# A graph-attention layer on one core: pair sums by single-input reduces, two buffers for near logits, and sums turned a batch later

## The chip, the core and the metric

The kernel runs on one core of a Trainium2 chip. The metric is the device time of one execution in microseconds (us), given as the median of several runs; it is to be as low as possible. The engines of the core work side by side, each in the order of its own instruction queue, and meet at semaphores: PE (matrix multiply), DVE (vector), ACT (scalar, and activations such as exp), POOL (general purpose; here it issues the gathers), and SP (here it issues loads). ACT also issues some DMAs.

## The reference, cut to what matters

A graph of N = 12500 nodes with 128 features and E = 412500 edges, sorted by their destination `tgt`. Every edge has 64 features. Attention has H = 4 heads of HD = 32.

```python
h = relu(layernorm(x))                                    # 12500 x 128
hn = (h @ W_node.T).reshape(N, H, HD)
e  = (edge_attr_64 @ W_edge.T).reshape(E, H, HD)
att = sum(concat([hn[src], hn[tgt], e], -1) * a, -1)      # E x H
att = where(att > 0, att, 0.2 * att)
m = maximum(segment_max(att, tgt), 0)
ex = exp(att - m[tgt])
denom = segment_sum(ex, tgt) + (E - deg)[:, None] * exp(-m)
out = x + segment_sum((ex / denom[tgt])[..., None] * hn[src], tgt)
```

So a logit is the sum of three parts: one of the source node, one of the destination node (below: the near logit, since destinations of neighbouring edges lie near each other) and one of the edge (below: z).

## The kernel before

**Tiling.** The edges are cut into 461 chunks of 896 (T = 7 tiles of 128), and 7 chunks make a batch: 66 batches. A table row in HBM holds 4 heads x 36 floats for each node: the 32 features of a head, a one, space, and the node's own logit. The loop of the program (L1121) runs over batches 0 to 64; the last batch, 65, is done in two parts behind it.

**One batch on the engines.** The queues' order is the order in which the functions are called in the loop, since each engine works its instructions in program order.

- *POOL* gathers the table rows of the batch's edges into one of RING = 4 buffers `hs` (L659): 49 indirect DMAs of 128 rows. Before each batch stands a memset of a tile called gate (L655), which waits until PE has finished the scatter of the batch that used the buffer last. In iteration b the gather of batch b+1 is issued, behind the scatter of batch b-3.
- *SP* loads, in iteration b, the near logits of batch b+1 (`load_near`, L605, 7 DMAs, each of which spreads one window of 32 nodes to all partitions), the node penalties of batch b+1 (L685; they mark where a node's edges begin) and the edge features of batch b+2 (`load`, L597).
- *PE* makes z of batch b+2 from the edge features at the end of iteration b (`begin`, L704 and L707, 14 matmuls).
- *ACT and DVE* pick each edge's near logit out of its window. ACT spreads the lower half of the window over all edges (`spread`, L618, tile `pick`); DVE halves it five times by predicated copies, by the bits of the edge's place (`choose`, L622 to L634). This is done in iteration b for batch b+1.
- *DVE and ACT* make the weights. `add_ends` adds the own logit and the near one (L758) and transposes (L760), so that a chunk and head lie on a partition; ACT copies the result to edge order (L763, four copies, one for each quadrant of 32 partitions). `highest_of` adds z (L771), applies the leak (L772, L773), finds the maximum of each node by two scans (L774, L776), subtracts it (L777) and forms a masked maximum (L778); four ACT copies (L780) take both results to `both`. `turn_weights` transposes back (L785), ACT takes exp (L790), and DVE writes the maxima into the rows (L791). `mark` (L716 to L722) writes the one-hot matrices of the scatter.
- *DVE and PE* scatter. DVE multiplies the rows by their weights (L859, three instructions) and adds tiles in pairs (L865, three adds), PE multiplies these sums by the one-hot matrices (L878, 10 products of 504 columns, each of which the trace shows as two matmuls). Where the two edges of a pair have different destinations, the second rows, masked by `split` (L868), are added up in two more adds (L870) and go through a correction matrix. PE accumulates all of it in `wide_ps`.
- *ACT* copies the accumulated sums of batch b-1 to `stage` (L886), writes them to HBM (`pass_on`, L887) and reads them back transposed (`turn_sums`, L900, 8 DMAs). `collect` (L915) waits for these and copies them into the input of the merge. Every two batches a merge on DVE (L946 to L988, called by `close`) joins neighbouring chunks' sums and adds them into the accumulators.

**Special places.** After batch COUNTED = 24 a count on DVE (L1006 to L1025) moves the accumulators' windows. From batch 62 on (`soon`) pass_on, turn_sums, collect and close are done for batch b itself in iteration b. Batch 65 takes `first_part` and `second_part`, which do not use `scatter` but multiply and add up chunk by chunk (L840, L847).

**Synchronization.** DMAs whose completion is counted by a semaphore of the kernel's own (near, pen, rows, wide, turned) are waited for by `landed`; all else is ordered by the framework, which makes a writer of a tile wait for its earlier readers, across engines by a semaphore.

Of the kernel before, what the change touches and what calls it, by code (L numbers as in the profile page):

```python
# [18 lines left out]
P = 128  # L19
# [50 lines left out]
PAIRS = ((0, 2), (2, 4), (4, T))  # L70
# [58 lines left out]
def kernel(  # L129
# [23 lines left out]
    wide = dram.tile([SB * BLOCK], F32, name="wide")  # L153
# [59 lines left out]
    lw = const.tile([P, CB, W * H], F32, name="lw")  # L213
# [14 lines left out]
    wide_sems, wide_done = [tc.alloc_semaphore("wide")], [0]  # L228
# [370 lines left out]
    def load_near(s):  # L599

        _, at = nc.values_load_multi_w_load_instructions(
            least_b[0:1, s.b, :s.chunks], engines=[ENG.SP], min_val=0, max_val=(NB * P - W) * NODE,
            skip_runtime_bounds_check_because="a dst is at most N, and N + W at most NB * P")
        for i, v in enumerate(at):
            by_itself(nc.sync.dma_start(  # L605
                lw[:, i, :].bitcast(U8),
                near_b[ds(v, W * NODE)].rearrange("(o c) -> o c", o=1).to_broadcast([P, W * NODE])),
                f"near{s.b}", near_sems, near_done, s.b % 2)

    def spread(s):  # L610

        landed(nc.scalar, f"near{s.b}", near_sems, near_done, s.b % 2, lw[:, :, :])
# [5 lines left out]
        nc.scalar.copy(s.pick[:, :, :s.chunks, :], lw[:, None, :s.chunks, :n].to_broadcast([P, T, s.chunks, n]))  # L618

    def choose(s):  # L620

        nc.vector.tensor_tensor(  # L622
# [51 lines left out]
    def landed(engine, group, sems, done, k, *what):  # L674

        wait = engine.wait_ge(sems[k], done[k], synchronizes=[engine.lower_ap(w) for w in what])
        if what:
            tc.declare_no_dep(wait.ins, group=group, reason="the semaphore counts these loads")
        tc.declare_fence(wait.ins, group=group)
# [67 lines left out]
    def grouped(s, what, g, t0, t1):  # L747

        order = "r w (t g i) -> r w g t i" if s.b == NBT - 1 else "r w (g i t) -> r w g t i"
        return what.rearrange(order, g=NQT, i=R)[:, :, g, t0:t1, :]  # L750
# [5 lines left out]
    def add_ends(s, t0, t1):  # L756

        nc.vector.tensor_tensor(logits[:, t0:t1, :s.chunks * H].rearrange("p t (q h) -> p t q h", h=H),  # L758
                                own_of(s, t0, t1), s.pick[:, t0:t1, :s.chunks, :H], op=OP.add)
        nc.vector.transpose(s.zst[:, t0:t1, :].rearrange("p t i -> p (t i)"),  # L760
                            logits[:, t0:t1, :].rearrange("p t i -> p (t i)"))
        for g in range(NQT):
            nc.scalar.copy(grouped(s, s.pair[:, 0:1, :], g, t0, t1)[:, 0], s.zst[g * R:(g + 1) * R, t0:t1, :])  # L763

    def highest_of(s, t0, t1):
# [5 lines left out]
        on_half(s, nc.vector.tensor_tensor(up[:, e0:e1], z, att[:, e0:e1], op=OP.add))  # L771
# [6 lines left out]
        nc.vector.scalar_tensor_tensor(mp, s.pen[:, e0 + 1:e1 + 1], -1.0 / BIG, up[:, e0:e1], op0=OP.mult, op1=OP.mult)  # L778
        for g in range(NQT):
            nc.scalar.copy(both[g * R:(g + 1) * R, :, t0:t1, :], grouped(s, s.pair, g, t0, t1))  # L780

    def turn_weights(s, t0, t1):
# [7 lines left out]
        nc.scalar.activation(ex_ps[:, t0:t1, :], ex_ps[:, t0:t1, :], AF.Exp)  # L790
# [35 lines left out]
    def second_part(s):  # L826
# [4 lines left out]
        r = work.tile([P, AW * (MC + 1)], F32, name="r")  # L831
        r = r[:, :AW * (len(spans) * s.chunks + 1)].rearrange("p (d c) -> p d c", d=AW)
        nc.scalar.copy(r[:, :, 1::len(spans)], s.first)
        nc.scalar.copy(r[:, :, 2::len(spans)], sum_part(s, *spans[1]))
        return r, s.breaks
# [16 lines left out]
    def scatter(s):  # L852
# [4 lines left out]
        for t0, t1 in PAIRS:  # L857
# [7 lines left out]
            nc.vector.tensor_tensor(tiles[:, t0, :], tiles[:, t0, :], tiles[:, t0 + 1, :], op=OP.add)  # L865
        add_to(s, t0, ROUNDS - 3)
        odd = s.hs.rearrange("p (t q) c -> p t q c", t=T)[:, 1::2, :, :]
        nc.vector.tensor_tensor(odd, odd, split_ps[:, :, :, None].to_broadcast([P, T // 2, CB, ROW]), op=OP.mult)  # L868
        for k in range(1, T // 2):
            nc.vector.tensor_tensor(tiles[:, 1, :], tiles[:, 1, :], tiles[:, 2 * k + 1, :], op=OP.add)  # L870
# [12 lines left out]
    def pass_on(s):  # L883
# [3 lines left out]
        by_itself(nc.scalar.dma_start(wide[:P * 2 * SPAN].rearrange("(p k) -> p k", p=P),  # L887
                                      s.stage.rearrange("p g c -> p (g c)")), f"wide{s.b}", wide_sems, wide_done, 0)

    def turn_sums(s):  # L890

        landed(nc.scalar, f"wide{s.b}", wide_sems, wide_done, 0)
# [12 lines left out]

    def collect(s):

        first, last = merge_of(s.b)
        if s.b == first:
            n = chunks_of(first, last)  # L910
            r = work.tile([P, AW * (MC + 1)], F32, name="r")
            merged[first] = r[:, :AW * (n + 1)].rearrange("p (d c) -> p d c", d=AW),
# [24 lines left out]
    def merge(b0, c0, count, r, breaks=None):  # L937

        n = count if breaks is None else 2 * count
# [7 lines left out]
        m = r[:, AW - 1, 1:n + 1]  # L947
        val = work.tile([P, CE], F32, name="up")[:, :AW * (n + 1)].rearrange("p (d c) -> p d c", d=AW)
# [6 lines left out]
        if not ended:  # L955
# [9 lines left out]
        nc.vector.tensor_copy(r[:, :AW - 1, 0], carry)  # L965
# [6 lines left out]
        part = r[:, :HD + 1, 1:n + 1]  # L972
        nc.vector.tensor_tensor(part, part, scale[:, None, :n].to_broadcast([P, HD + 1, n]), op=OP.mult)
        nc.vector.tensor_tensor_scan(val[:, :AW - 1, :].rearrange("p d c -> p (d c)"), f.rearrange("p d c -> p (d c)"),
                                     r[:, :AW - 1, :].rearrange("p d c -> p (d c)"), 0.0,
# [129 lines left out]
    with tc.manual_schedule():  # L1105
# [7 lines left out]
        load_near(batch(0))  # L1113
        load_pen(batch(0))
# [6 lines left out]
        for b in range(NBT - 1):  # L1121
# [5 lines left out]
            load_near(batch(b + 1))  # L1127
# [10 lines left out]
            if b + 2 < NBT:  # L1138
                open_rows(batch(b + 2))
            if b == NBT - 2:  # L1140
# [5 lines left out]
            if b < NBT - 2:  # L1146
                spread(batch(b + 1))
                mark(s)
# [32 lines left out]
            if soon:  # L1181
# [3 lines left out]
                collect(s)  # L1185
# [300 lines left out]
```

## Time and profile before

| | |
|---|---|
| median of 3 runs | 4788.1 us (4781.82 to 4800.94) |
| the profiled execution's own time | 4789.11 us |
| its span, from the first to the last instruction | 4787.3 us |
| busy: DVE | 3041.7 us (64%), 3240 instructions |
| busy: POOL | 3227.6 us (67%), 3394 instructions |
| busy: PE | 1287.3 us (27%), 2855 matmuls |
| busy: ACT | 801.2 us (17%), 988 instructions |
| mean granted clock of PE | 0.627 |
| gathers | 3223 indirect DMAs, 237.83 MB, 19.1% of the time of 16 DMA engines |

The profile shows one execution, instruction by instruction. A group is all instructions of one line of the code, engine and shape: its busy time, the mean duration of one in ns, the time the engine was idle just before them, and what ended most of that idle time ("<-DMA", another engine's instruction, "remote" for a semaphore whose sender the profile could not name, or "issue" where the engine waited for nothing that is shown). The timeline gives single instructions: start and duration in us, engine, line, and in brackets the idle time before and its releaser. Durations of PE are modelled at their ends. An engine with the suffix q is its instruction queue, here where it issues DMAs.

### The profile page before, as it was taken

Reading aid. Unit: us, or ns where it says so; the run is one execution under the profiler, and the core shown is the slowest. Engines: PE = TensorE matmul, PEld = TensorE weight load, DVE = VectorE, ACT = ScalarE, POOL = GpSimd, SP = SyncE. Lnnn points to the kernel's source line nnn. Section 1 sums busy time; section 2 is a strip of 40 time slices with the busy share of each in tenths; the row PEclk is TensorE's granted clock in tenths of the full one; section 3 lists DMA queues with packets and bytes.
Section 4 is the critical chain, followed back from the end, with each engine's and each line's share of the span. In section 5 each row is a group of like instructions: output and inputs, shape, how many; then the busy total and the mean of one; then the engine's idle time right before and its main releaser. Section 6 shows DMA issues by size and latency. Waiting matters only on the chain. (4 is left out here: it accounts for less than half of the span.)

```text
span 4787.3 us, 17028 instructions
## 1 busy us (share of the span) xinstructions
PE 1287.3 (27%) x2855; PEld 455.8 (10%) x2855; DVE 3041.7 (64%) x3240; ACT 801.2 (17%) x988; POOL 3227.6 (67%) x3394
## 2 busy tenths in 40 slices
PE   4312232222322314033321322322312313222221
PEld 3000010000100101011100100100100101010010
DVE  7644385586665767098945755846855748485576
ACT  3111021021111112022211211211211212121011
POOL 5777667667676767747776775775776767767630
PEclk7656566566656656566665666655656656566566
DMA  6433333343333424324342433333424323333330
GB/s 169 113 79 85 88 107 81 94 106 101 101 92 95 107 73 111 95 77 121 91 103 70 113 100 92 99 98 96 108 79 116 90 79 108 102 104 83 93 89 13
DMA packets 417217, 457.02 MB, mean 95 GB/s; under 512 B 240582, under 2 KB 324762, under 8 KB 417100
## 3 DMA queue, kind: packets, MB, share of 16 engines
q0 software_dynamic: 103136, 237.83, 19.1%
q1 hardware_dynamic: 199216, 165.73, 12.9%
q10 hardware_dynamic: 114748, 52.30, 4.1%
q14 instruction: 93, 0.76, 0.1%
q8 instruction: 24, 0.39, 0.0%
HBM read 406.51 MB, written 49.05 MB: 95 GB/s over the span
## 5 line engine op out<-in xcount | busy, mean ns | idle before, releaser
L659 POOL DMA_INDIRECT hs<-table,ends x3223 | 3193.1, 991 | 1009.9 <-issue 1002.7
L878 PE MATMUL pa<-hs,hot 128*128 128x504 f32 x1300 | 771.6, 753 | 2407.8 <-issue 791.8
L878 PEld LDWEIGHTS pa<-hs,hot 128*128 128x128 f32 x1300 | 301.3, 242 | 2841.3 <-issue 1877.1
L707 PE MATMUL z<-eft,wa 128*32 128x512 f32 (+1 forms) x792 | 377.6, 627 | 598.5 <-issue 389.6
L634 DVE COPY_PREDICATED pick<-more,lw 128x3136 f32<-128x3136 int32 x65 | 240.1, 3694 | 428.3 <-issue 324.1
L771 DVE TENSOR_TENSOR up<-z,a 32x896 f32<-32x896 f32 (+1 forms) x67 | 72.2, 1078 | 664.9 <-remote 512.8
L859 DVE TENSOR_TENSOR hs<-hs,exr 128x1848 f32<-128x1848 f32 (+1 forms) x195 | 466.5, 2392 | 0.0
L618 ACT COPY pick<-lw 128x3136 f32<-128x3136 f32 x65 | 182.3, 2805 | 1179.2 <-DMA lw<-near 948.5
L780 ACT COPY both<-a 32x448 f32<-32x448 f32 (+2 forms) x268 | 263.0, 982 | 247.8 <-DVE a L778 154.9
L634 DVE COPY_PREDICATED pick<-more,pick 128x1568 f32<-128x1568 int32 (+3 forms) x260 | 250.9, 965 | 8.9
L763 ACT COPY a<-zst 32x224 f32<-32x224 f32 (+2 forms) x268 | 155.6, 581 | 577.4 <-DVE logits L758 216.0
L865 DVE TENSOR_TENSOR hs<-hs 128x1008 f32<-128x1008 f32 x195 | 235.8, 1209 | 8.5 <-DVE hs L859 1.0
L655 POOL MEMSET gate<- 128x1 f32 x62 | 7.5, 121 | 339.8 <-remote 297.6
L868 DVE TENSOR_TENSOR hs<-hs,more 128x3024 f32<-128x3024 f32 x65 | 214.7, 3303 | 2.3
L704 PE MATMUL z<-eft,wa 128*64 128x512 f32 (+1 forms) x132 | 84.2, 727 | 375.8 <-issue 252.6
L707 PEld LDWEIGHTS z<-eft,wa 128*32 128x32 f32 x792 | 89.1, 123 | 920.8 <-issue 701.8
L886 ACT COPY stage<-pa 128x1008 f32<-128x1008 f32 x65 | 64.9, 998 | 609.0 <-remote 550.9
L870 DVE TENSOR_TENSOR hs<-hs 128x1008 f32<-128x1008 f32 x130 | 157.0, 1208 | 4.5
L986 DVE TENSOR_REDUCE up<-a 128x280 f32<-128x1960 f32 x66 | 145.1, 2198 | 4.2 <-DVE a L984 2.0
L984 DVE TENSOR_TENSOR a<-up,more 128x1960 f32<-128x1960 f32 x66 | 144.2, 2185 | 0.0
L774 DVE TENSOR_TENSOR_SCAN up<-pen_sb,z 32x896 f32<-32x896 f32 (+1 forms) x67 | 133.6, 1994 | 5.7 <-DVE z L773 2.6
L776 DVE TENSOR_TENSOR_SCAN a<-pen_sb,up 32x896 f32<-32x896 f32 (+1 forms) x67 | 132.6, 1979 | 2.3
(191 smaller groups left out, 1251.8 us busy)
## 6 DMA issues: line engine op xcount, KB each, us to landing
eft<-in_ef SPq DMA_DIRECT2D x33, 1792.0 KB
hs<-table,ends POOLq DMA_INDIRECT x3223
eft<-in_ef SPq DMA_DIRECT2D x33, 1344.0 KB
wide<-stage ACTq DMA_DIRECT2D x65, 504.0 KB
lw<-near SPq DMA_DIRECT2D x461, 64.0 KB
pen_sb<-pens SPq DMA_DIRECT2D x66, 98.1 KB
table<-rows ACTq DMA_DIRECT2D x9, 648.0 KB
xg<-in_x SPq DMA_DIRECT2D x52, 112.0 KB
```

What stands on the lines that cost most here:

```text
L618: nc.scalar.copy(s.pick[:, :, :s.chunks, :], lw[:, None, :s.chunks, :n].to_broadcast([P, T, s.chunks, n]))
L634: nc.vector.copy_predicated(s.pick[:, :, :s.chunks, :n], bit[:, :, :, None].to_broadcast([P, T, s.chunks, n]), more)
L659: load = nc.gpsimd.indirect_dma_start(out=s.hs[:, t * CB + q, :], out_offset=None, in_=table[:, :], in_offset=bass.IndirectOffsetOnAxis(ap ...
L707: s.made = own_half(s, nc.tensor.matmul(s.z[:, part], wa3[:, j + s.b % 2 * (SB + 1), :], s.eft[:, j, part], start=False, stop=(j == NEXT - ...
L763: nc.scalar.copy(grouped(s, s.pair[:, 0:1, :], g, t0, t1)[:, 0], s.zst[g * R:(g + 1) * R, t0:t1, :])
L780: nc.scalar.copy(both[g * R:(g + 1) * R, :, t0:t1, :], grouped(s, s.pair, g, t0, t1))
L859: nc.vector.tensor_tensor(rows, rows, ex_ps[:, t0:t1, :CB * H, None].to_broadcast([P, t1 - t0, CB * H, HB]), op=OP.mult)
L865: nc.vector.tensor_tensor(tiles[:, t0, :], tiles[:, t0, :], tiles[:, t0 + 1, :], op=OP.add)
L868: nc.vector.tensor_tensor(odd, odd, split_ps[:, :, :, None].to_broadcast([P, T // 2, CB, ROW]), op=OP.mult)
L870: nc.vector.tensor_tensor(tiles[:, 1, :], tiles[:, 1, :], tiles[:, 2 * k + 1, :], op=OP.add)
L878: scattered[s.b] = nc.tensor.matmul(wide_ps[:, g, :], s.hot[:, k, g * NEXT:g * NEXT + SB, :].rearrange("p q r -> p (q r)"), flat[:, at:at ...
L986: nc.vector.tensor_reduce(put, spread_out, AX.X, OP.add)
```

## The change

Four things are changed, all in the loop over batches.

1. *Sums in pairs.* `scatter` multiplies the odd seventh tile first and then the six others in one instruction. The three pair sums are made by one `tensor_reduce` over a view in which the two tiles of a pair are the innermost axis (4032 bytes apart), into `two`, which is the memory of `pick`; PE reads the pairs there. The rows that `split` has masked are summed by a second `tensor_reduce` (three tiles, 8064 bytes apart) into tile 0.
2. *No ACT copies around the weights.* z and the transposed logits are added by four DVE additions, one a quadrant, with the reordering in the views of the operands. ACT takes the exp of each quadrant on the way from `att` to `both`; DVE writes the masked maxima into `both` itself, by quadrant. The exp after the transpose goes. Since `pick` is now overwritten earlier, ACT copies the chosen near logits to a small tile `picked`, which L758 of the next iteration reads. `mark` is called behind `choose`.
3. *Near logits in two buffers.* `lw` becomes `lws` with two halves, and `load_near(b + 2)` is issued in iteration b behind the edge load of batch b+2, in place of `load_near(b + 1)` at its head.
4. *Sums turned an iteration later.* The HBM tile `wide` becomes four, the sums of batch b-2 (not b-1) are read back in iteration b, straight into the merge's input `turned`; `collect` goes, and DVE waits for the DMAs in `merge`, whose other tiles are rearranged for it.

```diff
-    lw = const.tile([P, CB, W * H], F32, name="lw")
+    lws = const.tile([P, 2, CB, W * H], F32, name="lws")
...
-                lw[:, i, :].bitcast(U8),
+                lws[:, s.b % 2, i, :].bitcast(U8),
...
+        s.picked = s.pick[:, :, :, :H]
+        if s.b < NBT - 1:
+            s.picked = work.tile([P, T, CB, H], F32, name="picked")
+            nc.scalar.copy(s.picked, s.pick[:, :, :, :H])
...
-                                own_of(s, t0, t1), s.pick[:, t0:t1, :s.chunks, :H], op=OP.add)
+                                own_of(s, t0, t1), s.picked[:, t0:t1, :s.chunks, :], op=OP.add)
...
-        for g in range(NQT):
-            nc.scalar.copy(grouped(s, s.pair[:, 0:1, :], g, t0, t1)[:, 0], s.zst[g * R:(g + 1) * R, t0:t1, :])
...
-        on_half(s, nc.vector.tensor_tensor(up[:, e0:e1], z, att[:, e0:e1], op=OP.add))
+        for g in range(NQT):
+            on_half(s, nc.vector.tensor_tensor(grouped(s, up, g, t0, t1), grouped(s, s.z, g, t0, t1),
+                                               s.zst[g * R:(g + 1) * R, t0:t1, :], op=OP.add))
...
-        nc.vector.scalar_tensor_tensor(mp, s.pen[:, e0 + 1:e1 + 1], -1.0 / BIG, up[:, e0:e1], op0=OP.mult, op1=OP.mult)
         for g in range(NQT):
-            nc.scalar.copy(both[g * R:(g + 1) * R, :, t0:t1, :], grouped(s, s.pair, g, t0, t1))
+            nc.scalar.activation(both[g * R:(g + 1) * R, 0, t0:t1, :], grouped(s, att, g, t0, t1), AF.Exp)
+        for g in range(NQT):
+            nc.vector.scalar_tensor_tensor(both[g * R:(g + 1) * R, 1, t0:t1, :], grouped(s, s.pen[:, 1:], g, t0, t1), -1.0 / BIG,
+                                           grouped(s, up, g, t0, t1), op0=OP.mult, op1=OP.mult)
...
-        nc.scalar.activation(ex_ps[:, t0:t1, :], ex_ps[:, t0:t1, :], AF.Exp)
...
-        for t0, t1 in PAIRS:
+        for t0, t1 in ((T - 1, T), (0, T - 1)):
             rows = blocks[:, t0:t1, :, :HB]
             nc.vector.tensor_tensor(
                 rows, rows, ex_ps[:, t0:t1, :CB * H, None].to_broadcast([P, t1 - t0, CB * H, HB]), op=OP.mult)
-            if t0:
-                add_to(s, t0 - 2, t0 // 2 - 1, t0 == 2)
             if t1 == T:
-                add_to(s, T - 1, ROUNDS - 2)
-            nc.vector.tensor_tensor(tiles[:, t0, :], tiles[:, t0, :], tiles[:, t0 + 1, :], op=OP.add)
-        add_to(s, t0, ROUNDS - 3)
+                add_to(s, T - 1, ROUNDS - 2, True)
+        pairs = flat[:, :(T - 1) * CB * ROW].rearrange("p (k j c) -> p k c j", j=2, c=CB * ROW)
+        two = pick.rearrange("p t q k -> p (t q k)")
+        nc.vector.tensor_reduce(two[:, :T // 2 * CB * ROW].rearrange("p (k c) -> p k c", k=T // 2), pairs, AX.X, OP.add)
+        for k in range(T // 2):
+            add_to(s, k, k, of=two)
         odd = s.hs.rearrange("p (t q) c -> p t q c", t=T)[:, 1::2, :, :]
         nc.vector.tensor_tensor(odd, odd, split_ps[:, :, :, None].to_broadcast([P, T // 2, CB, ROW]), op=OP.mult)
-        for k in range(1, T // 2):
-            nc.vector.tensor_tensor(tiles[:, 1, :], tiles[:, 1, :], tiles[:, 2 * k + 1, :], op=OP.add)
-        add_to(s, 1, ROUNDS - 1)
-
-    def add_to(s, t, k, start=False):
-
-        flat = s.hs.rearrange("p i c -> p (i c)")
+        seconds = flat.rearrange("p (t c) -> p c t", t=T)[:, :, 1::2]
+        nc.vector.tensor_reduce(tiles[:, 0, :], seconds, AX.X, OP.add)
+        add_to(s, 0, ROUNDS - 1)
+
+    def add_to(s, t, k, start=False, of=None):
+
+        flat = s.hs.rearrange("p i c -> p (i c)") if of is None else of
...
-        by_itself(nc.scalar.dma_start(wide[:P * 2 * SPAN].rearrange("(p k) -> p k", p=P),
-                                      s.stage.rearrange("p g c -> p (g c)")), f"wide{s.b}", wide_sems, wide_done, 0)
+        by_itself(nc.scalar.dma_start(wides[s.b % 4][:P * 2 * SPAN].rearrange("(p k) -> p k", p=P),
+                                      s.stage.rearrange("p g c -> p (g c)")), f"wide{s.b}", wide_sems, wide_done, s.b % 2)
+
+    def written(s):
+
+        landed(nc.scalar, f"wide{s.b}", wide_sems, wide_done, s.b % 2)
...
-        turned = work.tile([P, CB, AW], F32, name="turned")
-        s.sums = turned.rearrange("p q d -> p d q")
-        blocks = wide.rearrange("(q m) -> q m", q=SB)[:, :W * 2 * SPAN].rearrange("q (i k) -> i q k", i=W)
+        first, last = merge_of(s.b)
+        if s.b == first:
+            merged[first] = work.tile([P, MC, AW], F32, name="turned", bufs=2), None
+        at = s.c0 - chunk_of(first)
+        turned = merged[first][0][:, at:at + CB, :]
+        blocks = wides[s.b % 4].rearrange("(q m) -> q m", q=SB)[:, :W * 2 * SPAN].rearrange("q (i k) -> i q k", i=W)
...
-        landed(nc.scalar, f"turned{s.b}", turn_sems, turn_done, 0)
-        at = 1 + s.c0 - chunk_of(first)
-        nc.scalar.copy(merged[first][0][:, :, at:at + CB], s.sums)
...
+        if breaks is None:
+            groups = [f"turned{b}" for b in range(b0, merge_of(b0)[1] + 1)]
+            landed(nc.vector, groups, turn_sems, turn_done, 0, turned)
...
+        got_sums = turned[:, :n, :].rearrange("p c d -> p d c")
+        m = got_sums[:, AW - 1, :]
+        val = work.tile([P, AW * (MC + 1)], F32, name="val")[:, :AW * (n + 1)].rearrange("p (d c) -> p d c", d=AW)
...
+        nc.vector.tensor_copy(r[:, HD + 1, 1:], got_sums[:, HD + 1, :])
...
+        load_near(batch(1))
...
-            load_near(batch(b + 1))
...
+                load_near(batch(b + 2))
...
-                mark(s)
...
+                mark(s)
             turn_weights(s, 0, T)
+            if 2 <= b <= NBT - ALONE:
+                written(batch(b - 2))
             if 1 <= b <= NBT - ALONE:
                 pass_on(batch(b - 1))
             scatter(s)
-            if 1 <= b <= NBT - ALONE:
+            if 2 <= b <= NBT - ALONE:
+                turn_sums(batch(b - 2))
+            if b == NBT - ALONE:
+                written(batch(b - 1))
                 turn_sums(batch(b - 1))
             if 2 <= b < NBT - ALONE:
                 close(batch(b - 2))
-            if 1 <= b <= NBT - ALONE:
-                collect(batch(b - 1))
             if b == NBT - ALONE:
                 close(batch(b - 1))
             if soon:
                 pass_on(s)
                 if b == NBT - 2:
                     first_part(batch(b + 1))
+                written(s)
...
-                collect(s)
```

More of the change, by code (lines that the diff above doesn't have):

```diff
@@ L152 @@
     pens = dram.tile([NC2, CE + 1], F32, name="pens")
-    wide = dram.tile([SB * BLOCK], F32, name="wide")
+    wides = [dram.tile([SB * BLOCK], F32, name=f"wide{k}") for k in range(4)]
     ident = const.tile([P, P], F32, name="ident")
@@ L227 @@
     pen_done = [0, 0]
-    wide_sems, wide_done = [tc.alloc_semaphore("wide")], [0]
+    wide_sems, wide_done = [tc.alloc_semaphore(f"wide{k}") for k in range(2)], [0, 0]
     turn_sems, turn_done = [tc.alloc_semaphore("turned")], [0]
@@ L610, in spread @@
     def spread(s):
[L612 removed]
+        lw = lws[:, s.b % 2]
+        landed(nc.scalar, f"near{s.b}", near_sems, near_done, s.b % 2, lw)
         n = W * H // 2
@@ L676, in landed @@
         wait = engine.wait_ge(sems[k], done[k], synchronizes=[engine.lower_ap(w) for w in what])
-        if what:
-            tc.declare_no_dep(wait.ins, group=group, reason="the semaphore counts these loads")
-        tc.declare_fence(wait.ins, group=group)
+        for each in group if isinstance(group, list) else [group]:
+            if what:
+                tc.declare_no_dep(wait.ins, group=each, reason="the semaphore counts these loads")
+            tc.declare_fence(wait.ins, group=each)
         return wait.ins
@@ L830, in second_part @@
         weigh_part(s, *spans[1])
[L831 to L835, printed above, removed]
+        turned = work.tile([P, MC, AW], F32, name="turned", bufs=2)
+        by_part = turned[:, :len(spans) * s.chunks, :].rearrange("p (q k) d -> p k d q", k=len(spans))
+        nc.scalar.copy(by_part[:, 0], s.first)
+        nc.scalar.copy(by_part[:, 1], sum_part(s, *spans[1]))
+        return turned, s.breaks
     def multiply(s, q, t0, t1):
```

25 lines of the change are left out of this document (8 added, 17 removed).

## The prediction

> **What bounds the kernel now.** I read the groups of the page first, then the timeline of POOL's gate, then whole stretches between gates, then all engines around one late batch. In a group stand busy us, mean ns of one, idle us just before it, and what ended that idle time.
>
> ```profile
> span 4787.3 us, 17028 instructions
> ...
> L659 POOL DMA_INDIRECT hs<-table,ends x3223 | 3193.1, 991 | 1009.9 <-issue 1002.7
> ...
> L771 DVE TENSOR_TENSOR up<-z,a 32x896 f32<-32x896 f32 (+1 forms) x67 | 72.2, 1078 | 664.9 <-remote 512.8
> ...
> L618 ACT COPY pick<-lw 128x3136 f32<-128x3136 f32 x65 | 182.3, 2805 | 1179.2 <-DMA lw<-near 948.5
> ...
> L655 POOL MEMSET gate<- 128x1 f32 x62 | 7.5, 121 | 339.8 <-remote 297.6
> ```
>
> POOL issues 3223 gathers at (3193.1+1009.9)/3223 = 1.304 us, so the 49 of a batch take 63.9 us, and the gate that holds a batch until its ring buffer is free costs 339.8 us in all: together 4543 of the 4787.3 us. That looks like POOL's pace. The gate's own rows say otherwise. Between the waits below lie four, four and, from the fourth row to the fifth, six batches (62 gate rows in the trace, one a batch).
>
> ```profile
> 1244.14 0.10 POOL L655 MEMSET gate<- 128x1 f32 x1 [19.73 <-remote]
> 1519.43 0.10 POOL L655 MEMSET gate<- 128x1 f32 x1 [21.37 <-remote]
> 1794.76 0.10 POOL L655 MEMSET gate<- 128x1 f32 x1 [20.61 <-remote]
> 2224.64 0.10 POOL L655 MEMSET gate<- 128x1 f32 x1 [7.28 <-remote]
> 2637.11 0.10 POOL L655 MEMSET gate<- 128x1 f32 x1 [23.46 <-remote]
> ```
>
> That is 68.82, 68.83 and 68.75 us a batch. POOL's work in the first and in the last of these stretches differs (us, POOL busy on gathers, clock, DMA share, GB/s):
>
> ```profile
> 1244.14:1519.43 275.29, 193.75 (x196) 0.62 0.36 97
> 2224.64:2637.11 412.47, 294.39 (x294) 0.64 0.36 97
> ```
>
> A gather takes 0.989 us in one and 1.001 in the other, 0.63 us a batch apart, and the gate gives the difference back: it waited 20-odd us over four batches and over six. So **something behind the gate passes one batch per 68.8 us**, and POOL runs ahead of it until the ring is full. What it waits for shows in one late batch:
>
> ```profile
> 2543.55 10.53 PE L878 MATMUL pa<-hs,hot 128*128 128x504 f32 x19 [41.72 <-DVE more L969]
> 2586.59 0.41 SPq L597 DMA_DIRECT2D eft<-in_ef  x1
> 2586.66 1.09 DVE L771 TENSOR_TENSOR up<-z,a 32x896 f32<-32x896 f32 x1 [21.01 <-remote]
> 2592.86 17.49 SPq L605 DMA_DIRECT2D lw<-near  x7
> 2637.02 1.00 ACT L886 COPY stage<-pa 128x1008 f32<-128x1008 f32 x1 [16.20 <-remote]
> ```
>
> PE shows this batch's 20 scatter matmuls done by about 2556, yet ACT's stage copy and POOL's gate, which wait for the last of them, go at 2637.02 and 2637.11, 80 us later. DVE's L771 and SP's edge load, both behind z matmuls, go together at 2586.6. I read this as PE's completions, z and scatter alike, arriving in order and late. PE has 68 instructions a batch (40 scatter, 28 z, loads included), so 68.8 us is 1.01 us of each. What that rate is made of the trace doesn't tell; that no batch count, no merge and no POOL stretch moves it, it does. The change leaves all 68 in place.
>
> **The change part by part.** DVE rows, by shape:
>
> ```profile
> L859 DVE TENSOR_TENSOR hs<-hs,exr 128x1848 f32<-128x1848 f32 x130 | 269.2, 2071 | 0.0
> L859 DVE TENSOR_TENSOR hs<-hs,exr 128x2772 f32<-128x2772 f32 x65 | 197.3, 3036 | 0.0
> L865 DVE TENSOR_TENSOR hs<-hs 128x1008 f32<-128x1008 f32 x195 | 235.8, 1209 | 8.5 <-DVE hs L859 1.0 <-issue 0.9
> L870 DVE TENSOR_TENSOR hs<-hs 128x1008 f32<-128x1008 f32 x130 | 157.0, 1208 | 4.5
> L986 DVE TENSOR_REDUCE up<-a 128x280 f32<-128x1960 f32 x65 | 143.2, 2203 | 4.1 <-DVE a L984 2.0
> L986 DVE TENSOR_REDUCE up<-a 128x280 f32<-128x1680 f32 x1 | 1.9, 1911 | 0.0
> L791 DVE COPY hs<-exr 128x196 f32<-128x196 f32 x65 | 32.7, 504 | 26.7 <-issue 20.6 <-ACT exr L790 6.1
> L771 DVE TENSOR_TENSOR up<-z,a 32x896 f32<-32x896 f32 x65 | 71.0, 1092 | 659.7 <-remote 512.8 <-issue 84.1 <-ACT a L763 62.7
> L778 DVE SCALAR_TENSOR_TENSOR a<-pen_sb,up 32x896 f32<-32x896 f32 x65 | 69.8, 1075 | 2.2
> L763 ACT COPY a<-zst 32x224 f32<-32x224 f32 x260 | 153.3, 590 | 573.6 <-DVE logits L758 216.0 <-DVE zst L760 156.7 <-DVE dk L716 111.6
> ```
>
> *Multiplies.* Two of 1848 and one of 2772 elements become one of 924 and one of 5544. The two L859 rows give (3036-2071)/924 = 1.044 ns an element and 0.14 us fixed: 7.18 us before, 1.11+5.93 = 7.04 after.
>
> *Sums.* Five adds, 5 x 1.209 = 6.04 us, become two reduces that read 6048 and 3024 elements. The L986 rows give (2203-1911)/280 = 1.043 ns an element read, with neighbours adjacent: 6.47+3.31 = 9.78 us. Here the elements summed lie 4032 and 8064 bytes apart. The nearest row for a far stride is L791, which writes every 144 bytes: (504-160)/196 = 1.76 ns. At 1.7 ns the two take 10.4+5.3 = 15.7 us; at twice the contiguous rate 19.2. Nothing in the trace has a reduce read faster than 1.04, so a gain is excluded. With the multiplies: **+3.6, +9.5 or +13 us a batch**. I take +9.5, since what changes against L986 is just what sets L791 apart.
>
> [...]
>
> *Logits and weights.* ACT loses its four L763 copies (4 x 0.59) and L790; its four copies L780 become four exps. DVE takes over: one add of 896 becomes four of 224, and so does L778. At 1.04 ns and 0.16 us fixed, four cost 1.56 us against 1.09; at 1.7 ns, 2.15. So +0.5 to +1.1 each, +2.1 taken for both.
>
> *DVE's sum* is about +11.6 us a batch (+4.6 to +15). DVE is busy 64% of the span, 46 us a batch (3041.7/66); at 58 it still fits under 68.8, and while PE is the late one DVE's added work falls into its waits before L771. Gone cover would cost the whole 11.6 in each batch.
>
> *Near logits in two buffers.* SP's queue is edge load b+1, near b+1 before and after: the near load stood at the head of iteration b, right behind the edge load that iteration b-1 issued, and now stands right behind it in iteration b-1, past the node-penalty load and an index load. In the rows SP's near issue starts 6 us after the edge load that PE's late z let go, not after a wait for the buffer. I count nothing. Its seven issues, their register loads and the transfer remain, so ACT's 948.5 us for near loads remain.
>
> *Sums an iteration later.* ACT no longer waits for the transposing DMAs, and the collecting copy L915 goes; DVE gets the wait at each merge, with the next batch queued behind it, but the data are a whole batch old. POOL is passed by nothing. Zero in the body. The `picked` copy (some 0.5 us) goes to ACT, which is 17% busy.
>
> *Where DVE's work is on the path.* First at the accumulators' count in batch 25, then after the last gather. (L1006 and what follows hold DVE until here; POOL stands at its gate for this very batch.)
>
> ```profile
> 2044.73 0.49 DVE L758 TENSOR_TENSOR logits<-hs,pick 128x196 f32<-128x196 f32 x1 [0.26 <-DVE total L1025]
> ...
> 2087.49 0.10 POOL L655 MEMSET gate<- 128x1 f32 x1 [41.89 <-PE pa L878]
> ```
> ```profile
> 4557.83 2.81 ACT L618 COPY pick<-lw 128x3136 f32<-128x3136 f32 x1 [44.65 <-DMA lw<-near]
> ...
> 4695.43 1.09 DVE L771 TENSOR_TENSOR up<-z,a 32x896 f32<-32x896 f32 x1 [2.49 <-ACT a L763]
> ...
> 4709.22 0.66 DVE L785 STREAM_TRANSPOSE exr<-both 128x448 f32<-128x448 f32 x1 [4.15 <-ACT both L780]
> ```
>
> From 2044.7 to the gate everything is DVE with PE behind it: 11.6 less a microsecond of waits for ACT, +10 us. In the tail DVE is at work nearly throughout from the copy at 4557.83 on. Batches 62 and 63 wait under 1 us for ACT's copies: +11 each. Batch 64 loses 2.5 (L763), about 2.7 of the 4.15 (four exps of one plane instead of copies of two) and L790's 0.4: 11.6-5.6 = +6. The last batch runs no reduce and loses two waits for L763: -2 by the same row, halved for its smaller tiles. The collecting copies (0.6 each) and their hand-overs before the last merges: -2. Tail +24.
>
> **The sum.** The profiled execution took 4789.1 us (span 4787.3 and 1.8 around it), 1.0 above the median of 4788.1 and inside 4781.8 to 4800.9. 4789 + 10 + 24 = **4823 us**. With the contiguous rate (4.6 in place of 11.6 wherever it stands) it is 4789+4+3 = 4796, with 19.2 us of reduces 4789+14+34 = 4837. A difference under 0.5%, 24 us, can hardly be told from none here, so up to 4812 counts as no change.
>
> **The rivals.**
>
> *Faster: the adds hold up POOL, and POOL sets the pace.* Beside an add of two inputs a gather stretches:
>
> ```profile
> 1836.03 0.94 POOL L659 DMA_INDIRECT hs<-table,ends  x1 [0.30 <-issue]
> ...
> 1840.01 1.68 POOL L659 DMA_INDIRECT hs<-table,ends  x1 [0.31 <-issue]
> ```
> ```profile
> 1839.66 1.21 DVE L865 TENSOR_TENSOR hs<-hs 128x1008 f32<-128x1008 f32 x1
> ```
>
> 0.991 less 0.94 is 0.05 us, times 3223 some 160 us, most of it beside the five adds that go. If a batch follows POOL, 4789-160+34 = 4663. Against it stands the even 68.8: it did not follow 0.63 us of POOL. [...] Less likely still, the gate waits vanish too, 4789-340-160+34 = 4323.
>
> *Slower by much: the pairs' tile closes a loop.* The pair sums go into `pick`, so ACT's spread of the next batch must wait until PE has read them, and by the rows PE's word comes up to 80 us late; the exps are queued behind the spread on ACT, the weights' transpose waits for them on DVE, then the reduces, then PE. One turn is spread 2.8, choosing 8, mark 2, transpose and copy 1, multiplies 7, pairs 10.4, together 31 us, then word of PE's 28 instructions up to the pairs' last. From L771 to the stage copy in the late batch word of 40 came in 50.4 us, 1.26 each: 35 us, and the next batch's 28 z instructions need another 35, more than the 31 that they could lie beside. It decides where that passes 68.8: 70 to 71 us a batch, over 62 batches +75 to +135, so 4898 to 4958 with the +34. For it: the lateness of 80 us. Against it: a slower loop feeds PE less, and the lateness shrinks.
>
> *No change that can be measured: the reduces run at L986's rate.* About 4796. For it: the only reduces in the trace. Against it: their inputs are adjacent.
>
> **How the numbers follow.** The forecast, pace held and strided reduces (4802 to 4838), 0.36; contiguous rate 0.18; the loop 0.22; POOL freed 0.20; gate waits gone as well 0.04. The range from 4655 to 4925 takes in the unknown rates, POOL freed and the better half of the loop; it leaves out the loop's worse half, the case without gate waits and some of POOL freed, not quite 0.2. Faster by over 0.5%: 0.24. Within: 0.18 and a fifth of the forecast's chance, 0.25. Slower: 0.51.
>
> **What would show it.** Right, if gates with a wait still stand 68.8 us a batch apart, the pair reduce takes near 10.4 us and the one of the seconds near 5.3, the gathers' mean falls to about 0.95 and the gate's idle time grows by as much. Wrong by the first rival, if batches come at 66 to 67 us; by the loop, if L618 waits for PE and batches come above 70; by the third, if the reduces take 6.5 and 3.3 us.

## The result, and the profile after

The changed kernel took 4826.9 us (median of 7 runs, 4815.9 to 4847.4), the kernel before 4788.1 in the same runs: 1.0087 times, 95% interval 1.0060 to 1.0115. The prediction was 4823. The number fits; the way to it does so only in part, and the experiments show that the same change has the other sign elsewhere. The kernel before takes 4780 to 4793 us on some chips (the first measurement, e5, e6, e12) and 4318 us on others (the other nine runs), so every run is compared with the kernel before on its own chip, and the first kind is called late below (PE's word, the signal that its products are done, comes up to 85 us late there, and at once in e4 and e9; the rows stand in the part on the prediction), the second prompt.

The page of the changed kernel, the groups that answer to those shown of before:

```profile
span 4818.2 us, 16923 instructions
...
L664 POOL DMA_INDIRECT hs<-table,ends x3223 | 3066.2, 951 | 1012.6 <-issue 1006.7
...
L618 ACT COPY pick<-lws 128x3136 f32<-128x3136 f32 x65 | 182.3, 2805 | 2394.8 <-remote 1815.1
...
L660 POOL MEMSET gate<- 128x1 f32 x62 | 6.8, 110 | 493.1 <-remote 424.4
```

Three things are to be seen. A gather takes 0.951 us in place of 0.991, so POOL has 3223 x 0.04 = 127 us less to do. The gate's idle time rises from 339.8 to 493.1 us, by 153: **all that POOL gained was waited away, and some more**. And ACT's spread, which used to wait for near loads (948.5 us), now waits 1815 us for something "remote"; PE is named for 260 us more, as in the last row of ACT and SP below, and in e9 for 674 of 728 us.

The gate on POOL's timeline:

```profile
324.40 0.37 POOL L660 MEMSET gate<- 128x1 f32 x1
...
2108.95 0.10 POOL L660 MEMSET gate<- 128x1 f32 x1 [46.85 <-PE pa L885]
...
2523.78 0.10 POOL L660 MEMSET gate<- 128x1 f32 x1 [22.64 <-remote]
2662.19 0.10 POOL L660 MEMSET gate<- 128x1 f32 x1 [15.26 <-remote]
2800.67 0.10 POOL L660 MEMSET gate<- 128x1 f32 x1 [14.53 <-remote]
...
4596.41 0.10 POOL L660 MEMSET gate<- 128x1 f32 x1 [15.33 <-remote]
```

The waits now come mostly every second batch, and the three rows from 2523.78 on lie two batches apart: 69.2 us a batch, against 68.8 before, although the gathers of a batch are 2 us shorter. The first and the last gate of the kernel before:

```profile
326.93 0.11 POOL L655 MEMSET gate<- 128x1 f32 x1
...
4564.81 0.10 POOL L655 MEMSET gate<- 128x1 f32 x1 [13.40 <-remote]
```

From the last gate to the end it is 4818.2-4596.4 = 221.8 us, before 4787.3-4564.8 = 222.5. So the 31 us between the spans are -2.5 up to the first gate, +24 from there to the gate behind the count (2108.95 against 2087.49), +10 in the 36 batches behind it, and nothing in the tail.

What the gate waits for, on ACT and SP of the changed kernel around the first of these waits:

```profile
2482.32 0.41 SPq L596 DMA_DIRECT2D eft<-in_ef  x1
2485.08 17.50 SPq L604 DMA_DIRECT2D lws<-near  x7
...
2523.63 2.81 ACT L618 COPY pick<-lws 128x3136 f32<-128x3136 f32 x1 [49.90 <-remote]
2523.81 0.41 SPq L596 DMA_DIRECT2D eft<-in_ef  x1
2560.51 2.81 ACT L618 COPY pick<-lws 128x3136 f32<-128x3136 f32 x1 [25.06 <-PE pa L885]
```

At 2523.6 to 2523.8 ACT's spread, POOL's gate and SP's edge load go together: one waits for PE's pair products, one for the scatter's last product, one for the z products that still read the edge features. The spread of the following batch has PE named outright, and of all the 2395 us of idle time before the spreads only 3.5 are still put down to near loads.

DVE's new steps, by shape:

```profile
L871 DVE TENSOR_REDUCE pick<-hs 128x3024 f32<-128x6048 f32 x65 | 424.8, 6536 | 6.6
L865 DVE TENSOR_TENSOR hs<-hs,exr 128x5544 f32<-128x5544 f32 x65 | 384.5, 5916 | 0.0
...
L877 DVE TENSOR_REDUCE hs<-hs 128x1008 f32<-128x3024 f32 x65 | 235.2, 3619 | 2.2
...
L786 DVE SCALAR_TENSOR_TENSOR both<-pen_sb,up 32x224 f32<-32x224 f32 x260 | 141.0, 542 | 50.0 <-issue 46.6
...
L775 DVE TENSOR_TENSOR up<-z,zst 32x224 f32<-32x224 f32 x260 | 102.1, 393 | 228.7 <-issue 102.2 <-remote 101.6 <-DVE up L775 13.4
...
L865 DVE TENSOR_TENSOR hs<-hs,exr 128x924 f32<-128x924 f32 x65 | 71.8, 1104 | 0.0
```

The pair reduce takes 6.54 us, the one of the seconds 3.62: (6536-160)/6048 = 1.05 and (3619-160)/3024 = 1.14 ns an element read, with the 160 ns that the L986 rows leave as fixed. L986, whose inputs are adjacent, reads at 1.04: the stride of 4032 bytes added 0.01 ns, that of 8064 bytes 0.10.

### The profile page after: what moved, and what is told of

Read it like the earlier page. It is cut to its first block, busy times and chain, and to the rows that moved or that the text cites. A ratio compares the mean times of both kernels' runs of the same rounds, so it can differ in the third digit from the quotient of the medians.

```text
span 4818.2 us, 16923 instructions
## 1 busy us (share of the span) xinstructions
PE 1341.5 (28%) x2855; PEld 476.4 (10%) x2855; DVE 3430.4 (71%) x3417; ACT 497.8 (10%) x653; POOL 3100.4 (64%) x3394
## 5 line engine op out<-in xcount | busy, mean ns | idle before, releaser
L885 PE MATMUL pa<-hs,hot 128*128 128x504 f32 x520 | 359.4, 830 | 2198.5 <-DVE hs L865 1391.4
L635 DVE COPY_PREDICATED pick<-more,lws 128x3136 f32<-128x3136 int32 x65 | 239.8, 3689 | 722.4 <-ACT pick L618 611.1
L885 PE MATMUL pa<-pick,hot 128*128 128x504 f32 x780 | 488.3, 792 | 558.9 <-DVE pick L871 306.0
L865 DVE TENSOR_TENSOR hs<-hs,exr 128x924 f32<-128x924 f32 (+1 forms) x130 | 450.9, 3510 | 0.0
L618 ACT COPY pick<-lws 128x3136 f32<-128x3136 f32 x65 | 182.3, 2805 | 2394.8 <-remote 1815.1
L871 DVE TENSOR_REDUCE pick<-hs 128x3024 f32<-128x6048 f32 x65 | 424.8, 6536 | 6.6
L885 PEld LDWEIGHTS pa<-hs,hot 128*128 128x128 f32 x520 | 123.9, 257 | 2374.5 <-issue 2223.8
L660 POOL MEMSET gate<- 128x1 f32 x62 | 6.8, 110 | 493.1 <-remote 424.4
L885 PEld LDWEIGHTS pa<-pick,hot 128*128 128x128 f32 x780 | 197.9, 264 | 893.1 <-issue 535.8
L877 DVE TENSOR_REDUCE hs<-hs 128x1008 f32<-128x3024 f32 x65 | 235.2, 3619 | 2.2
L784 ACT ACTIVATE both<-a 32x224 f32<-32x224 f32 (+2 forms) x268 | 159.1, 594 | 414.8 <-DVE a L782 264.7
```

Source lines behind the costliest of these rows:

```text
L784: nc.scalar.activation(both[g * R:(g + 1) * R, 0, t0:t1, :], grouped(s, att, g, t0, t1), AF.Exp)
L865: nc.vector.tensor_tensor(rows, rows, ex_ps[:, t0:t1, :CB * H, None].to_broadcast([P, t1 - t0, CB * H, HB]), op=OP.mult)
L871: nc.vector.tensor_reduce(two[:, :T // 2 * CB * ROW].rearrange("p (k c) -> p k c", k=T // 2), pairs, AX.X, OP.add)
L877: nc.vector.tensor_reduce(tiles[:, 0, :], seconds, AX.X, OP.add)
L885: scattered[s.b] = nc.tensor.matmul(wide_ps[:, g, :], s.hot[:, k, g * NEXT:g * NEXT + SB, :].rearrange("p q r -> p (q r)"), flat[:, at:at ...
```

## The experiments

**e1 and e8: the change without its reduces.** In the changed kernel `scatter` is that of before.

```diff
-        for t0, t1 in ((T - 1, T), (0, T - 1)):
+        for t0, t1 in PAIRS:
...
-        nc.vector.tensor_reduce(two[...], pairs, AX.X, OP.add)
+            nc.vector.tensor_tensor(tiles[:, t0, :], tiles[:, t0, :], tiles[:, t0 + 1, :], op=OP.add)
```

> The changed kernel with the five adds of before put back (L859 to L870 as before), everything else of the change kept: no reduce, and ACT's spread no longer waits for PE. If the body is held at about 68.8 us a batch by PE's late word and the change costs only through DVE's own additions, this loses only the +2 us a batch of the split steps where DVE is on the path and gains the ACT copies in the tail: about 0 to -10 us against before, and the gathers stretch again to about 0.99 us. If the wait of the spread for PE (the loop) is what cost the 39 us, it also comes back to before, but then the batches of the changed kernel must lie further apart than here. If near loads, ACT steps or late sums cost time of their own, it stays 20 us or more above before.

> The changed kernel with the five adds of before. Where before takes about 4790 us: if near loads, ACT steps and late sums are neutral and only the reduces with their loop cost, within 0.3% of before and below the changed kernel; if they carry the cost, the same 4810 to 4827 as the changed kernel; if they help the late word (fewer ACT steps behind it) and the reduces' loop takes it back, 1% or more below before. Where before takes 4318 us: +15 again.

Measured: 4333.0 against 4318.3 us, 1.0036 (1.0022 to 1.0050), and 4335.9 against 4318.3, 1.0043 (1.0027 to 1.0060). Both fell on prompt chips, where the gate of before never waits, so what e1 was to decide between the rivals of a late chip stays undecided. In e1's page:

```profile
span 4330.5 us, 17089 instructions
...
L665 POOL DMA_INDIRECT hs<-table,ends x3223 | 3218.2, 999 | 984.7 <-issue 984.7
```

Here POOL sets the pace, and a gather takes 0.999 us (before on such a chip 0.992, e4): 3223 x 0.007 = 22 us more, 8 less elsewhere. So near loads, ACT steps and late sums save no time by themselves there; they move DVE's adds to places where they hold up the gathers a little more: the gathers that lie for the longest part beside a pair add take 1.60 us in the mean in e1 (L872, 50 of them) and 0.96 in e4 (L868, 64).

**e2, e7 and e11: fewer PE instructions.** The kernel before, with one z product a half in place of three (z leaves out two thirds of the edge part).

```diff
-            for j in range(NEXT):
+            for j in range(1):
...
-                    start=False, stop=(j == NEXT - 1), skip_group_check=True))
+                    start=False, stop=True, skip_group_check=True))
```

> The kernel before with one product in place of three a half in begin (L707), so z leaves out two thirds of the edge part: 52 PE instructions a batch in place of 68. Theory A, PE's word sets the pace at about 1.01 us an instruction: POOL becomes the bound, batches 64 us apart, gate waits near 0, about -280 us. Theory B, POOL's issuing with fixed waits behind it sets it: no change beyond 0.5%. Theory C, the chain of DVE and ACT sets it: no change.

> The kernel before with one z product in place of three a half (z leaves out two thirds of the edge part; 52 PE instructions a batch in place of 68). Where the kernel before takes about 4790 us, gates wait and PE's word is late: theory A, a rate of about 1 us for each PE instruction, gives a POOL-bound 64 us a batch and about 4330 to 4500 us. Theory D, the lateness has a length of its own that does not follow the number of PE instructions (some 60 us whenever POOL issues), gives within 1% of 4790. Where before takes 4318 us: no change, as in the first run of this kernel.

> The kernel before with one z product in place of three a half (z leaves out two thirds of the edge part; 52 PE instructions a batch in place of 68). Where before takes about 4790 us: theory A gives about 4330 to 4500 us, theory E within 1% of before, since the products that go signal nobody. Where before takes 4318 us: no change.

Measured: 0.9996 (0.9986 to 1.0006), 0.9999 (0.9989 to 1.0008) and 0.9999 (0.9988 to 1.0011). All three fell on chips with 4318 us, where no gate waits and PE's word is not late, so theory A had nothing to act on, and e2's -280 us were expected for the other kind of chip. Whether fewer PE instructions would help where PE's word is late has not been seen; these runs neither show nor refute theory A, and rows of the kernel before speak against it (below, on PE's word).

**e3: more work for DVE.** The kernel before, with the masking of the seconds done three times.

```diff
-        nc.vector.tensor_tensor(odd, odd, split_ps[...], op=OP.mult)
+        for _ in range(3):
+            nc.vector.tensor_tensor(odd, odd, split_ps[...], op=OP.mult)
```

> The kernel before with the masking of the second rows (L868) done three times, which adds 6.6 us of DVE a batch and no other wait. Theory A: the body keeps 68.8 us a batch, the added work shows only at the count (batch 25) and in the last three batches, 4 x 6.6 = +26 us. Theory C, DVE's chain sets the pace: 6.6 us on each of 65 batches, up to +400 us. Between them, half of the batches: +200.

Measured: 4328.5 against 4318.3 us, 1.0023 (1.0012 to 1.0034), for 65 x 6.6 = 429 us of added DVE work, on a prompt chip. The last gate of e3 and of e4 (which equals before in time):

```profile
4190.18 0.12 POOL L655 MEMSET gate<- 128x1 f32 x1
```
```profile
span 4318.4 us, 17090 instructions
...
L662 POOL DMA_INDIRECT hs<-table,ends x3223 | 3196.1, 992 | 985.4 <-issue 985.2
...
L761 DVE TENSOR_TENSOR logits<-hs,pick 128x196 f32<-128x196 f32 x65 | 32.4, 498 | 1021.9 <-DVEq L679 1021.9
```
```profile
4204.97 0.12 POOL L658 MEMSET gate<- 128x1 f32 x1
```

From the last gate on, e3 needs 4328.0-4190.2 = 137.8 us and e4 113.4: +24, between three and four times 6.6, as DVE's work in the last batches should cost. Up to the gate e3 is even 15 us earlier: its gathers take 3181.7 us in all against e4's 3196.1. In the body DVE waits 1022 us for gathers (the idle time before L761), and added work goes there. On a late chip this was not run.

**e4: the loop alone.** The kernel before, with ACT's spread made to wait for PE's scatter of the batch before last.

```diff
+        if 2 <= s.b < NBT - 1:
+            tc.add_manual_dep(spreading.ins, scattered[s.b - 2].ins.name, ...)
```

> The kernel before, with one wait added: ACT's spread for batch b+1 waits until PE has finished the scatter of batch b-1, as it does in the changed kernel through the shared tile (there only up to the pairs). If the loop is what costs: +35 to +130 us, the batches 69.3 to 71 us apart. If PE's word sets the pace anyway and the wait only moves idle time from one engine to another: within 0.5% of before.

Measured: 4318.0 against 4318.3 us, 1.0000 (0.9990 to 1.0009). In e4's page:

```profile
L618 ACT COPY pick<-lw 128x3136 f32<-128x3136 f32 x65 | 182.3, 2805 | 11.8 <-DVE more L628 10.3
```

The added wait never ended last here: ACT comes to its spread only behind the copies of L766, when PE's word has already come (1539.8 us of idle time stand before those copies, 11.8 before the spreads). So e4 shows little of the loop of the changed kernel, where those copies are gone; that this one costs nothing on a prompt chip is seen in e9. Neither e4 nor the loop by itself was run where the word is late.

**e5 and e6: both kernels again.**

> The changed kernel itself, beside the kernel before. In the four runs so far the kernel before took 4318 us, not 4788, its gates never waited, and PE's word came at once: POOL alone set the pace, 63.5 us a batch. If the lateness of PE's word is what held both kernels to 69 us a batch in the first profiles, then where it is absent the changed kernel follows POOL, whose gathers take 0.951 us in place of 0.991: about 62 x 2 = -125 us in the body, +5 in the tail, so about 4200. If the change slows by its own work (reduces, loop), it is 10 to 40 us above before here too. Where the lateness is there again, +39 as in the first measurement.

> The kernel before, for its profile on this chip: gates without waits, 63.5 us a batch and 4318 us if the lateness of PE's word is absent; 68.8 us and 4788 if it is there.

They fell on a chip with late words: 4808.9 against 4792.6 us, 1.0045 (1.0014 to 1.0076). Groups of e5 first, then of e6:

```profile
L664 POOL DMA_INDIRECT hs<-table,ends x3223 | 3063.4, 950 | 1018.1 <-issue 1013.1
...
L660 POOL MEMSET gate<- 128x1 f32 x62 | 6.7, 109 | 468.7 <-remote 384.1
```
```profile
L659 POOL DMA_INDIRECT hs<-table,ends x3223 | 3190.4, 990 | 1006.2 <-issue 1000.0
...
L655 POOL MEMSET gate<- 128x1 f32 x62 | 7.5, 120 | 325.1 <-remote 325.1
```

The same exchange: 127 us of gathers gone, 144 us of waits come. It repeats on a second measurement, with +16 us in place of +39.

**e9: the changed kernel on a chip with prompt words.**

> The changed kernel. Where before takes 4318 us, with gates that never wait: about 4200, since its gathers take 0.951 in place of 0.992 us (62 batches x 2 us) and nothing waits for PE. Where before takes about 4790: +15 to +40 again.

Measured: 4193.2 against 4318.3 us, **0.971 (0.9693 to 0.9726)**. Its page and its gates:

```profile
span 4192.6 us, 16923 instructions
...
L664 POOL DMA_INDIRECT hs<-table,ends x3223 | 3061.2, 950 | 984.7 <-issue 983.2
...
L618 ACT COPY pick<-lws 128x3136 f32<-128x3136 f32 x65 | 182.1, 2802 | 727.9 <-PE pa L885 673.8
```
```profile
321.60 0.12 POOL L660 MEMSET gate<- 128x1 f32 x1
4070.29 0.12 POOL L660 MEMSET gate<- 128x1 f32 x1
```

No gate waits, and a batch takes (4070.3-321.6)/61 = 61.5 us: 49 gathers at (3061.2+984.7)/3223 = 1.255 us. The gathers are as short as in the first profile after (0.951), but here the time follows them: 42 ns x 3223 = 135 us less than in e4. ACT still waits 674 us for PE before its spreads, at no cost. What becomes of a gather beside the second adds of e4 and beside the pair reduce of e9:

```profile
2337.55 2.45 DVE L873 TENSOR_TENSOR hs<-hs 128x1008 f32<-128x1008 f32 x2
2337.80 1.78 POOL L662 DMA_INDIRECT hs<-table,ends  x1 [0.30 <-issue]
```
```profile
2323.72 6.51 DVE L871 TENSOR_REDUCE pick<-hs 128x3024 f32<-128x6048 f32 x1
2324.84 0.95 POOL L664 DMA_INDIRECT hs<-table,ends  x1 [0.30 <-issue]
```

Over the whole traces, the gathers that lie for the longest part beside L873 take 1.51 us in the mean (94 of them), those beside the pair reduce 0.944 (334). Together with e1 and e8, which lack only the new scatter (the reduces, with the multiplies cut as one tile and six and the pairs in `pick`), this shows that the gain is the reduces'; the reduces without the rest of the change were not run. A gather in the trace of e9 with nothing of DVE beside it takes 0.944 us too. The trace of before has the same: 0.945 us with nothing of DVE beside the gather (1071 of them), 0.944 beside L986's reduce (110), 1.75 beside L870's adds (53).

**e10 and e12: fewer semaphore events.** The traces of chips with 4318 us also record the increments of semaphores nearly in full (78,444 in e4), those of the late ones some 10,800. So a second theory, E, was that the path of these events itself is full. The sums of two heads (e10), then of one head (e12, shown), are read back in place of four; the other heads' output is left out, and their part of `turned`, now one tile for all batches, stays zero.

```diff
-        for h in range(H):
+        for h in range(1):
...
+    turned = work.tile([P, CB, AW], F32, name="turned")
+    nc.vector.memset(turned, 0.0)
```

> The kernel before with the sums of two of the four heads read back transposed in place of all (4 DMAs a batch in place of 8; the other two heads' output is left out). The trace of a run with 4318 us records 78,444 semaphore events, some 1190 a batch, 128 of them from these DMAs; the traces with 4790 us record only some 10,800. Theory E, where the word is late it is the path of the semaphore updates itself that is full, and it passes a batch's 1190 in 68.8 us: 64 fewer give -3.7 us a batch, about -200 us where before takes 4790 us. Theory A, PE's instructions set the pace: no change there. Where before takes 4318 us: no change by either.

> The kernel before with the sums of one of the four heads read back transposed (2 DMAs a batch in place of 8; the other three heads' output is left out), which takes away 96 of some 1190 semaphore events a batch and no instruction of PE. Where before takes about 4790 us: theory E (the path of semaphore updates is full) gives 68.8 x 96/1190 = -5.6 us a batch, about 4450; theory A (PE's instructions) no change. Where before takes 4318 us: within 0.2% by either.

Measured: e10 4314.2 against 4318.4 us, 0.9990 (0.9978 to 1.0001), on a prompt chip, as either theory has it. e12 fell on a late one: 4769.3 against 4779.7 us, 0.9975 (0.9953 to 0.9996). Its gates, four and five batches apart:

```profile
1314.48 0.10 POOL L655 MEMSET gate<- 128x1 f32 x1 [21.01 <-remote]
1590.40 0.10 POOL L655 MEMSET gate<- 128x1 f32 x1 [21.72 <-remote]
...
2211.09 0.10 POOL L655 MEMSET gate<- 128x1 f32 x1 [21.74 <-remote]
2556.43 0.10 POOL L655 MEMSET gate<- 128x1 f32 x1 [22.74 <-remote]
```

69.0 and 69.1 us a batch, as before, where theory E wanted 63. **Theory E falls** as it was priced, with one rate for all events. The gathers' own events, an estimated 784 of the 1190 a batch (49 at the 16 that the trace of before shows for each of its first loads), are as many as before, so a limit on these alone is not excluded.

## Why the prediction was right, and where it was not

*What bounds the kernel.* This step held. That something behind the gate passes a batch in about 68.8 us, whatever POOL's gathers take, is what the result shows: with gathers 2 us a batch shorter it was 69.1 to 69.2, and the gate took the difference. This step carries the sign, and it is the step that depends on the chip: in e9 nothing stands behind the gate, and the rival "the adds hold up POOL" happens, 125 us of the 160 that it was given. Those 160 us suppose that a reduce stretches no gather; e9 shows 0.944 us beside the pair reduce.

*That it is PE's word.* The engines that wait for PE do so, and at 2523.6 to 2523.8 the spread, the gate and the edge load go together. That PE's 68 instructions at 1.01 us each are the rate was only argued, and rows of the kernel before, on both sides of the gate's wait that ends at 2637.11, speak against it:

```profile
2499.70 2.12 PE L707 MATMUL z<-eft,wa 128*32 128x384 f32 x6
...
2638.07 11.47 PE L878 MATMUL pa<-hs,hot 128*128 128x504 f32 x20 [38.94 <-ACT stage L886]
2639.54 3.84 SPq L605 DMA_DIRECT2D lw<-near  x7
...
2653.95 2.12 PE L707 MATMUL z<-eft,wa 128*32 128x384 f32 x6
...
2663.08 0.40 SPq L597 DMA_DIRECT2D eft<-in_ef  x1
```

The z that ended at 2501.8 let SP's edge load go at 2586.59, 85 us later; the one that ended at 2656.1, after POOL's pause at the gate, did so 7 us later. From 2638.07 on PE did all 68 instructions of a batch, and by 2663.08 their word had come: 0.37 us each, not 1.01. Through the whole trace this delay grows to 75 or 85 us while POOL issues and falls at a gate's wait; in e4 and e9 it is 0.0 in every batch. So **the lateness builds up while POOL issues and goes when POOL pauses**; it is not a fixed time for each PE instruction. What fills up, and what fixes 68.8, stays open; no run changed the number of gathers.

*The reduces: a term that was mis-sized.* The prediction took 1.7 ns an element, 15.7 us; measured were 1.05 and 1.14 ns, 10.2 us. With the multiplies (7.02) the scatter costs +4.0 us of DVE a batch, not +9.5, so the third rival had the rate. The row L791, a strided write at 1.76 ns, was the wrong neighbour; L986, the only reduce, at 1.04, was the right one. No run shows a reduce at 1.7 ns or at twice the contiguous rate, the prediction's 19.2 us.

*Logits and weights.* 4 x 0.393 and 4 x 0.542 us in place of 1.09 and 1.08: +1.6 us, predicted +2.1. DVE's sum is +5.5 us a batch, predicted 11.6.

*Count and tail.* At the count the way from the first step of batch 25 to the gate grew by 7 us (predicted 10). DVE's row there, against 2044.73 before:

```profile
2058.99 0.50 DVE L764 TENSOR_TENSOR logits<-hs,picked 128x196 f32<-128x196 f32 x1 [0.26 <-DVE total L1032]
```

Up to this row the changed kernel had already lost 14 us, which the prediction put at nothing; what took them is not shown. The tail was to cost 24 us and cost -0.7. By the prediction's own fast branch the sum would have been about 4796, so the 4823 came near 4826.9 by **two errors that cancel**: some 27 us too much at the count and in the tail, most of it for the reduces, and 24 too little for the other batches before the last gate. The sign was foreseen; that the size fits is luck, and on a prompt chip the sign would have been the other one.

*The loop.* The spread does wait for PE, 1815 us in place of the near loads' 949, and the waits fall on every second batch. It gave 69.1 to 69.2 us a batch, not the 70 to 71 at which that rival would have decided. Whether these 0.3 us a batch are the loop's is not shown: the change with the pair sums in a tile of their own was not run.

*Near loads in two buffers.* As predicted, no gain: the seven issues still start behind the edge load that PE lets go and take up to 18.2 us, as before. That ACT's 948.5 us for them would remain was wrong; the spread now waits for PE instead.

## What to carry to other kernels

When an engine looks like the bound, divide the time between its waits by the work between them: if that quotient does not move when the engine's own work does, relieving the engine buys only longer waits. Here it stayed at 68.8 us a batch with gathers of 0.989 and of 1.001 us, and 127 us less of gathers brought 153 us more of waits at the gate. Take the rate of a new instruction from a row of the same kind before a row with the same access pattern: here 1.05 and 1.14 ns came, near L986's 1.04 and not L791's 1.76. And measure a change on more than one chip: this one is worth 1.0087 or 0.971, by whether another limit stands behind the one that it lifts.

## What the runs showed of the hardware that was not expected

The same kernel takes 4318 us on three chips and about 4790 on others, with PE's granted clock nearly the same (0.644 in e4, 0.627 in the first profile). On the late ones SP's own instructions are slow too, by spells. SP's part of a near load, in the kernel before, before and after the gate's wait that ends at 2637.11 (least, median and longest time in ns):

```profile
L605 SPq MOVE lw<-near x7: 691/691/700, 2592.1 to 2607.6; - x7
```
```profile
L605 SPq MOVE lw<-near x7: 29/29/38, 2639.5 to 2642.9; - x7
```

A move of a register, for which no wait is recorded, takes 0.69 us in one batch and 0.03 in the next. Of the 66 near loads of that trace 49 take over 10 us and 12 under 5; eleven of these twelve begin within 4.5 us of the end of a gate's wait, the twelfth after the last gather. In e9 such a load is short:

```profile
2345.76 3.49 SPq L604 DMA_DIRECT2D lws<-near  x7
```

On prompt chips the page can also pair gathers with their landing (2.6 us in e4 and e9), which it cannot on the late ones. On those, 69 us a batch came in every kernel that was run there, with 2 us less of gathers (e5) and with 96 fewer semaphore events a batch (e12). What sets them apart is not known from these runs. Every time on record comes with a span and a clock from the profiler, so it is also open whether the recording has a part in it.
